# Merged mask matmuls and a later division in two attention blocks

## The chip, the cores and the metric

The kernel runs on one core of a Trainium2 chip. The metric is the device time of one launch in microseconds. The core has five engines with a queue each: TensorE (PE in the profile), VectorE (DVE), ScalarE (ACT), GpSimd (POOL) and SyncE (SP), which issues the transfers. Matmul results lie in PSUM, everything else on the chip in SBUF.

## The reference

Four blocks are applied in turn to `x` of 4 x 1024 x 128 (batches, tokens, channels). Each adds `s * silu(ffn(xn))` to `x`, where `xn` is the layer norm of `x` and `s` an attention or state-space result on `xn`:

```python
xn = _layernorm(x, axis=-1)
s = _L0_attn_ref(xn, ...)           # windowed causal attention, 16 heads of 8, window of 250 keys
g = _silu(_L0_ffn_ref(xn, ...))     # channel mix
x = x + s * g
xn = _layernorm(x, axis=-1)
s = _L1_attn_ref(xn, ...)           # causal attention, 16 heads of 8
g = _silu(_L1_ffn_ref(xn, ...))     # mixture of 8 experts
x = x + s * g
...                                 # block 2: full attention; block 3: state space and local attention
```

In blocks 0 and 1 a query at position t sees the keys up to t, in block 0 only the last 250 of them. Scores of other keys are masked before the softmax.

## The kernel before, in words

All of blocks 0 to 2 run through one function, `_attention`, with the mode `window`, `causal` or `full`. It works in units: a unit is one batch and four of the 16 heads (16 units per block). Tokens are cut into tiles of 128. A unit has two passes.

The first pass, `maxima`, finds the largest score of each query. For a query tile `qt` the queries lie on the 128 PSUM partitions and the keys along the row. PE multiplies `q9` with `k9` (bf16, results in `max_ps`), then adds the mask to the same PSUM words by a matmul of the identity `ident16` with a tile of 0 and -1e30 (`k.mask[mode]`). DVE reduces the row to a negative maximum, `neg` (L344). One `max_ps` tile is two PSUM banks, 1024 words a row, and there are two such buffers. It holds four heads where a head's keys fit into 256 words (query tiles 0 and 1, pitch 128 and 256), two heads at pitch 512 and one at pitch 1024. In window mode a head of query tile 2 or later has 384 keys. Both of its edges need masking: the first 134 keys and the last 128. Tile 0 has 128 keys, tile 1 has 256, of which the first 6 and the last 128 are masked. In causal mode only the last 128 keys are masked. POOL splits `neg` into three bf16 parts (`negp`), PE transposes them (`neg_ps`), DVE copies them out (`negr`), and three transfers on SP put them as rows into `q9`.

The second pass, `attend`, takes blocks of 128 keys against up to 512 queries (half `hf` 0 or 1 of the tokens). For each block and pair of heads PE computes scores (`sc`, one bank each), ACT takes the exponential into `pt` (L417), and POOL zeroes what lies beyond the edges (`keep`, L387). Two blocks later (`lag` is 2 in blocks 0 and 1, 1 in block 2) `values` multiplies by the values and accumulates in `o_ps`, of which there is a single buffer. After a half's last block, DVE copies `o_ps` to `os` (L448). Then `normalize` transposes `os` on PE to `ot`, and DVE takes the reciprocal of the sums (`rec`, L460) and multiplies (`at`, L461). `ot`, `sc`, `neg_ps` and several others share three PSUM slots of one bank each.

Units overlap. While unit n attends, the maxima of units n+1 and n+2 are computed. `_interleave` merges the lists of steps in a fixed ratio, together with the projections of the next batch and the layer norms and routing for the next block (`plan`). The end of a unit (its last values, the second half's division, and after a batch's last unit the four `finish` steps: transposition and output projection) is inserted into the next unit's list at fixed places. PE keeps this order exactly. The program's scheduler arranges DVE's and POOL's instructions among themselves.

```python
            def second(hn=hn, i=i):
                if i >= lag:
                    values(*blks[i - lag])
                pair.pop(hn)(1)
                if i > lag and blks[i - lag - 1][0] < blks[i - lag][0]:
                    normalize(0)
```

Here the first half is divided one block after its last values. The second half's division is inserted at place 5 of the next unit's list, its values at places 1 and 3.

The masks are built once at the start by POOL: a memset and one or two selects each (L1897, L1900), ahead of other memsets and of the first layer norm's `ln_rs`.

## Time and profile before

| | us |
|---|---|
| median of three runs | 3613.82 (3608.35 to 3614.92) |
| the profiled execution: its time | 3610.66 |
| its span in the profile | 3608.9 |
| PE busy with matmuls | 3138.7 (87%), 24592 of them |
| DVE busy | 2445.6 (68%) |
| ACT busy | 1988.7 (55%) |
| POOL busy | 1417.2 (39%) |
| mask matmuls of block 0 (`max_ps<-mask_window`) | 960, first at 67.2, last at 525.0 |
| mask matmuls of block 1 (`max_ps<-mask_causal`) | 512, first at 615.3, last at 1327.4 |

In the lines of the timeline the first number is the start in the span, the second the time from the first start to the last end of the merged instructions. A matmul's duration includes its drain, so several may be busy at once; the distance between starts tells how fast they stream. Square brackets tell how long the engine had been idle and what ended that. In the table by stretches the columns are busy us and instructions of each engine, then the granted TensorE clock (1 is full speed), the share of transfer time and GB/s. `PEld` is the weight load, which overlaps with matmuls.

### The profile page before, as it was taken

How to read it: one execution, taken by the hardware profiler on the slowest of the kernel's cores; microseconds unless marked ns; L12 is line 12 of the kernel's file. 1: busy time of each engine (PE TensorE's matmuls, PEld its weight loads, DVE VectorE, ACT ScalarE, POOL GpSimd, SP SyncE). 2: the span in 40 equal slices, each digit the busy share in tenths (PEclk: the TensorE clock that was granted, in tenths of full speed). 3: DMA queues.
4: the chain of work that ended last, by engine and by line, in shares of the span. 5: the costliest groups of instructions: out<-in, count | busy, mean ns of one | idle time of the engine just before them, and what ended most of it. 6: DMA issues, size and time to landing. Idle time of an engine off the chain costs nothing. (4 is left out here: it accounts for less than half of the span.)

```text
span 3608.9 us, 64740 instructions
## 1 busy us (share of the span) xinstructions
PE 3138.7 (87%) x24592; PEld 1704.4 (47%) x24729; DVE 2445.6 (68%) x4927; ACT 1988.7 (55%) x4191; POOL 1417.2 (39%) x1962
## 2 busy tenths in 40 slices
PE   4889889999898986899999989677499999989897
PEld 3545446654343433433323333223366666666665
DVE  7667664457777752788786766652587888778785
ACT  2444453346555552366665665554366666666674
POOL 5555552012323223030321300211576667656663
PEclk8999999999999997999999999888699999999999
DMA  3322312112222102011111221100210111010110
GB/s 99 71 60 55 70 42 83 46 33 51 57 42 57 34 22 69 21 44 28 41 34 33 55 53 31 33 19 9 78 22 18 21 25 24 18 25 22 29 26 21
DMA packets 133083, 146.09 MB, mean 40 GB/s; under 512 B 80403, under 2 KB 107931, under 8 KB 125467
## 3 DMA queue, kind: packets, MB, share of 16 engines
q1 hardware_dynamic: 130724, 137.75, 16.0%
q0 software_dynamic: 2048, 4.20, 0.4%
q8 instruction: 196, 3.21, 0.4%
q14 instruction: 115, 0.93, 0.1%
HBM read 93.83 MB, written 30.11 MB: 34 GB/s over the span
## 5 line engine op out<-in xcount | busy, mean ns | idle before, releaser
L417 ACT ACTIVATE pt<-sc 128x512 f32<-128x512 f32 (+3 forms) x2432 | 1077.0, 511 | 786.1 <-PE sc L78 737.7
L344 DVE TENSOR_REDUCE neg<-max_ps 128x1 f32<-128x1024 f32 (+6 forms) x1088 | 1177.9, 1102 | 477.2 <-PE max_ps L78 424.1
L78 PE MATMUL sc<-q,k 128*128 128x512 bf16 (+3 forms) x2403 | 651.8, 342 | 126.2 <-ACT pt L417 70.0
L78 PE MATMUL max_ps<-k,q 128*128 128x512 bf16 (+3 forms) x2198 | 625.0, 350 | 86.2 <-DVE neg L344 39.5
L78 PE MATMUL o_ps<-pt,va 128*32 128x512 f32 (+3 forms) x4864 | 560.6, 527 | 19.9 <-POOL pt L387 10.2
L387 POOL TENSOR_SCALAR_AFFINE_SELECT pt<-pt 128x256 f32<-128x256 f32 (+2 forms) x768 | 292.3, 399 | 568.2 <-ACT pt L417 566.3
L78 PEld LDWEIGHTS <-k 128*128 128x128 bf16 x2432 | 183.0, 98 | 544.2 <-issue 418.1
L78 PEld LDWEIGHTS <-q 128*128 128x128 bf16 x2304 | 222.7, 99 | 359.6 <-issue 241.2
L168 POOL CAST negp<-neg 128x32 bf16<-128x32 f32 x48 | 10.2, 212 | 719.3 <-DVE neg L344 719.2
L1603 ACT ACTIVATE pr<-lsc,nb,r 128x128 f32<-128x128 f32 x512 | 202.7, 476 | 61.2 <-DVE nb L1595 57.6
L1524 POOL TENSOR_TENSOR qn<-qn,rot 128x512 f32<-128x512 f32 x128 | 164.9, 1294 | 139.8 <-DVE rot L1516 125.9
L1533 POOL TENSOR_TENSOR rn<-ss,neghalf 128x16 f32<-128x16 f32 x64 | 188.9, 2951 | 68.8 <-DVE ss L1531 59.3
L78 PEld LDWEIGHTS o_ps<-pt,va 128*32 128x32 f32 x4864 | 99.7, 109 | 213.8 <-issue 160.3
L691 ACT ACTIVATE h<-hp,eb 128x512 f32<-128x512 f32 x128 | 80.9, 684 | 197.8 <-PE hp L78 190.2
L78 PEld LDWEIGHTS <-ident 128*128 128x128 bf16 x1472 | 146.2, 100 | 87.5 <-issue 22.7
L1441 PE MATMUL qk_ps<-wqkv,hT 128*128 128x512 f32 x256 | 137.9, 623 | 24.9 <-DVE hT L1487 10.3
L78 PE MATMUL hp<-xT,ew 128*128 128x512 f32 x256 | 130.3, 634 | 19.7 <-ACT rope_t L234 9.3
L701 DVE SCALAR_TENSOR_TENSOR xn<-op,gates,xn 128x128 f32<-128x128 f32 x256 | 72.1, 344 | 100.4 <-PE op L78 100.4
L78 PEld LDWEIGHTS op<-ew,h 128*128 128x128 f32 x1024 | 123.6, 192 | 20.1 <-issue 17.0
L78 PE MATMUL max_ps<-mask_window,ident 128*128 128x134 bf16 (+2 forms) x960 | 132.0, 221 | 0.0
L78 PE MATMUL op<-ew,h 128*128 128x128 f32 x1024 | 125.3, 276 | 0.0
L65 POOL TENSOR_TENSOR ln_rs<-ln_ve,neghalf 128x4 f32<-128x4 f32 x72 | 73.7, 1025 | 113.1 <-DVE ln_ve L63 109.7
(347 smaller groups left out, 5452.9 us busy)
## 6 DMA issues: line engine op xcount, KB each, us to landing
q<-qx SPq DMA_DIRECT2D x144, 192.0 KB
k<-kx SPq DMA_DIRECT2D x432, 64.0 KB
va<-vb SPq DMA_DIRECT2D x120, 128.0 KB
x<-x SPq DMA_DIRECT2D x20, 512.0 KB
qx<-qp SPq DMA_DIRECT2D x12, 768.0 KB
kx<-kp SPq DMA_DIRECT2D x12, 768.0 KB
ew<-in_e1w_dram SPq DMA_DIRECT2D x64, 128.0 KB
x<-in_x_dram SPq DMA_DIRECT2D x8, 512.0 KB
```

What stands on the lines that cost most here:

```text
L65: nc.gpsimd.tensor_tensor(rs, ve, k.neghalf[:, :n], ALU.pow)
L78: k.tc.keep_in_program_order(k.nc.tensor.matmul(*args, **kw))
L168: eng.tensor_copy(dst[:, 0], src)
L344: nc.vector.tensor_reduce(neg[:, j0 : j0 + m, qt0], of, AX.X, ALU.max, negate=True)
L387: nc.gpsimd.affine_select(out=pt, in_=pt, pattern=[[0, 2], [step, pt.shape[2]]], compare_op=ALU.is_ge, fill=0.0, base=base, channel_multip ...
L417: nc.scalar.activation(pt[:, j % 2, :width], sc[:, :width], AF.Exp, scale=scale)
L691: nc.scalar.activation(h[:, hh, :], hp[:, hh, :], AF.Gelu, bias=eb1[:, e, hh : hh + 1])
L701: nc.vector.scalar_tensor_tensor(to, op[:, c, :], gates[:, 4 * n + c, e : e + 1], to, ALU.mult, ALU.add)
L1441: pin(nc.tensor.matmul(*args, **kw))
L1524: nc.gpsimd.tensor_tensor(qn[:, i], qn[:, i], rot, ALU.add)
L1533: nc.gpsimd.tensor_tensor(rn, ss.rearrange("p w h -> p (w h)"), k.neghalf[:, : 2 * NH], ALU.pow)
L1603: nc.scalar.activation(t.pr[:, h, :], t.sc[r][:, c, :], AF.Exp, bias=t.nb[r][:, c : c + 1], scale=t.r8[:, h : h + 1])
```

## The change

The masks of a unit are added by fewer matmuls. For query tile 0, where four heads share a bank, one matmul adds the mask to all four (the mask is read four times by a step of zero). For tile 1, two heads share a bank and one matmul serves both; in window mode it covers all 256 keys of each. For window tiles from 2 on, one matmul per head writes the two edges as two runs of 134 words, 250 words apart. Both mask tiles are now allocated 512 columns wide in the pool `upto3`, and the causal mask is filled over 384 columns.

The division of a half moves one block of keys later in blocks 0 and 1 (`late` is 1 there, 0 in block 2): the first half's to the block after, the second half's from place 5 to place 7 of the next unit's list. The `finish` steps move by two places too.

```diff
+                pitch = parts[1][2] if len(parts) > 1 else 1024
...
-                        if masked:
-                            mw = min(c1 - c0, k.mask[mode].shape[1])
-                            W = k.mask[mode].shape[1]
-                            spans = [(W - P, W)]
-                            if W - mw < W - CONTEXT:
-                                spans.insert(0, (W - mw, W - CONTEXT))
-                            for m0, m1 in spans:
-                                matmul(
-                                    flat[:, at + c1 - c0 - W + m0 : at + c1 - c0 - W + m1],
-                                    lhsT=k.ident16,
-                                    rhs=k.mask[mode][:, m0:m1],
...
+                        if mode == "full" or c1 < hi or pitch < 512 and (place + pitch) % 512:
+                            continue
+                        mask = k.mask[mode]
+                        if mode == "window" and width == 3 * P:
+                            two = lambda a: a.rearrange("p (g c) -> p g c", c=CONTEXT)[:, :, 0 : 3 * P - CONTEXT]
+                            to, rhs = two(flat[:, at : at + 2 * CONTEXT]), two(mask[:, 0 : 2 * CONTEXT])
+                        else:
+                            heads = 512 // pitch if pitch < 512 else 1
+                            mw = width if mode == "window" else P
+                            b0 = at - at % 512 if pitch < 512 else at
+                            end = (c1 - c0) if pitch >= 512 else width
+                            to = flat[:, b0 : b0 + heads * end].rearrange("p (h c) -> p h c", h=heads)[:, :, end - mw : end]
+                            rhs = mask[:, 3 * P - mw : 3 * P].unsqueeze(1).to_broadcast([P, heads, mw])
+                        matmul(to, lhsT=k.ident16, rhs=rhs, start=False, stop=True, skip_group_check=True)
...
+    late = 0 if mode == "full" else 1
...
-                if i > lag and blks[i - lag - 1][0] < blks[i - lag][0]:
+                if i > lag + late and blks[i - lag - late - 1][0] < blks[i - lag - late][0]:
                     normalize(0)
...
-                for i in range(lag + 1):
-                    weights.insert(1 + 2 * i, late[i])
-                for i, step in enumerate(late[lag + 1 :]):
-                    weights.insert(min(len(weights), 2 * lag + 4 + 3 * i), step)
+                for i in range(lag):
+                    weights.insert(1 + 2 * i, left[i])
+                weights.insert(2 * lag + 1 + 2 * late, left[lag])
+                for i, step in enumerate(left[lag + 1 :]):
+                    weights.insert(min(len(weights), 2 * lag + 4 + 2 * late + 3 * i), step)
...
-    for name, width, reach in (("causal", P, None), ("window", 3 * P, CONTEXT)):
-        m = k.mask[name] = const.tile([P, width], BF16, name=f"mask_{name}")
+    for name, width, reach in (("causal", 3 * P, None), ("window", 3 * P, CONTEXT)):
+        k.mask[name] = upto3.tile([P, 4 * P], BF16, name=f"mask_{name}")
+        m = k.mask[name][:, 0:width]
```

More of the change, by code (lines that the diff above doesn't have):

```diff
@@ L315, in step @@
                         at = place + c0 - lo
-                        masked = mode != "full" and c1 == hi
                         matmul(
@@ L321, in step @@
                             start=True,
-                            stop=not masked,
+                            stop=mode == "full" or c1 < hi,
                             skip_group_check=True,
                         )
-                        if masked:
-                            mw = min(c1 - c0, k.mask[mode].shape[1])
-                            W = k.mask[mode].shape[1]
-                            spans = [(W - P, W)]
-                            if W - mw < W - CONTEXT:
-                                spans.insert(0, (W - mw, W - CONTEXT))
-                            for m0, m1 in spans:
-                                matmul(
-                                    flat[:, at + c1 - c0 - W + m0 : at + c1 - c0 - W + m1],
-                                    lhsT=k.ident16,
-                                    rhs=k.mask[mode][:, m0:m1],
-                                    start=False,
-                                    stop=m1 == W,
-                                    skip_group_check=True,
-                                )
+                        if mode == "full" or c1 < hi or pitch < 512 and (place + pitch) % 512:
[12 more added lines that the diff above has]
+                        matmul(to, lhsT=k.ident16, rhs=rhs, start=False, stop=True, skip_group_check=True)
                 j0, m = parts[0][0], len(parts)
@@ L526, in rest @@
         nonlocal steps, ending
-        late = []
+        left = []
         for n, (b, g) in enumerate(order):
@@ L545, in rest @@
                 streams.append((coming[:3], coming[3:7], coming[7:])[g])
-            if late:
-                for i in range(lag + 1):
-                    weights.insert(1 + 2 * i, late[i])
-                for i, step in enumerate(late[lag + 1 :]):
-                    weights.insert(min(len(weights), 2 * lag + 4 + 3 * i), step)
+            if left:
+                for i in range(lag):
[3 more added lines that the diff above has]
+                    weights.insert(min(len(weights), 2 * lag + 4 + 2 * late + 3 * i), step)
             _interleave(*streams, *plan.get(n, []))
-            late = closing + (finish(b) if g == 3 else [])
-        _run(late)
+            left = closing + (finish(b) if g == 3 else [])
+        _run(left)
     return begin, rest
```

## The prediction

> **What bounds the kernel now.** I read the table by stretches first, then the waits of TensorE (PE) in the two stages that the edit touches, then short timelines. Blocks 0 and 1 hold windowed attention (about 115 to 556 us) and causal attention (about 800 to 1364 us). The static order of the changed program differs from the old one in these two stages alone: from block 2 on every engine has the same order, and ACT's and SP's never change.

> ```profile
> core 0: us, PE busy (x) PEld busy (x) DVE busy (x) ACT busy (x) POOL busy (x), PEclk, DMA share, GB/s
> 180.00:270.00 90.00, 79.93 (x737) 43.66 (x736) 56.00 (x81) 41.70 (x125) 53.53 (x124) 0.98 0.27 60
> 810.00:900.00 90.00, 85.62 (x639) 37.24 (x648) 67.98 (x88) 54.09 (x132) 26.98 (x59) 1.00 0.24 51
> 2610.00:2700.00 90.00, 89.42 (x1094) 65.91 (x1086) 72.86 (x210) 55.53 (x133) 67.31 (x65) 0.96 0.11 24
> ```

> PE is the busiest engine of both stages (80 and 86 of 90 us), DVE comes next in the second. But PE's busy time includes the drain of its matmuls. Walking the trace from start to start, and counting each bf16 matmul at its column time (the timelines below), the streams fill 299 of the 415 us between 115 and 530, and 410 of the 550 between 780 and 1330. The rest is PE standing at the head of its queue. The profile names part of that, the window stage first, the causal stage second:

> ```profile
> PE sc L78 <- ACT pt L417: 14.6, 46, 0.6
> PE o_ps L78 <- POOL pt L387: 8.1, 5, 2.2
> PE ot L82 <- DVE os L448: 4.6, 4, 2.3
> ...
> PE sc L78 <- ACT pt L417: 15.6, 37, 3.0
> PE sc L78 <- DVE at L461: 13.7, 3, 4.6
> PE ot L82 <- DVE os L448: 3.6, 10, 0.6
> ```

> The columns are total us, times, longest. The change can reach the `ot` rows and the `at` row, not the `pt` rows, which are the larger.

> **Part 1, the masks.** Per unit (four heads; 16 units in each block) the windowed masks fall from 60 matmuls to 27, the causal ones from 32 to 27; with as many weight loads that is 608 matmuls and 608 loads fewer. What counts is columns:

> ```profile
> 123.55 0.27 PE L78 MATMUL max_ps<-k,q 128*128 128x256 bf16 x1
> 123.66 0.24 PE L78 MATMUL max_ps<-mask_window,ident 128*128 128x6 bf16 x2
> 123.74 0.27 PE L78 MATMUL max_ps<-k,q 128*128 128x256 bf16 x1
> ...
> 301.47 0.33 PE L78 MATMUL max_ps<-k,q 128*128 128x384 bf16 x1
> 301.63 0.28 PE L78 MATMUL max_ps<-mask_window,ident 128*128 128x134 bf16 x2
> 301.75 0.33 PE L78 MATMUL max_ps<-k,q 128*128 128x384 bf16 x1
> ```

> From one head's score to the next is 0.28 us: 0.16 for 384 columns and 0.12 for masks of 134 and 128. So a mask streams at 0.42 ns per column plus about 2.5 ns, and its weight load is hidden.
> - Query tiles 2 to 7 (24 heads per unit): 262 columns in two matmuls, 114 ns, become 268 in one, also 114 ns. Nothing.
> - Tile 0: four masks of 128 become one of 512. Nothing (-6 ns).
> - Tile 1: from head to head is 0.19 us, 0.76 for four. After, four scores of 0.109 and two masks of 512 columns, 0.216 each: 0.87. So +0.11 us per unit, +1.7 us over 16: the merged mask also streams the zeros.
> - Causal: the same columns everywhere, five matmuls fewer per unit, -0.2 us in all.

> The masks are also built at the start: the causal one grows from 128 to 384 columns, so its memset from 0.20 to 0.41 us and its select from 0.29 to 0.50 (the rows of the window mask). POOL runs without a gap from there to the first `ln_rs` at 16.72, for which DVE waits: +0.4 us on the path. Sum of part 1: +1.9 us.

> [...] No row here writes two runs. The nearest reads them: the `shift_ps` matmuls fetch 4 runs of 64 fp32 and take 379 ns for 256 columns, as do those of `o_ps` whose 256 are contiguous (379). [...] I take the row: 0 ns. [...]

> [...]

> **Part 2, the division.** `os` is copied by DVE out of `o_ps`, then PE transposes it (`ot`), then DVE divides (`rec`, `at`) and only then is the PSUM slot of `ot`, one of three that scores use, free. The second half's division is issued in the next unit right after its last value block, so PE meets a copy that is not done:

> ```profile
> 509.99 0.49 PE L78 MATMUL sc<-q,k 128*128 128x384 bf16 x2
> 512.76 0.63 PE L82 MATMUL ot<-ident,os 128*128 128x128 f32 x4 [2.27 <-DVE os L448]
> ```

> Before this `ot` PE stood still for 2.4 us. Taking the 62 divisions of the two blocks that have a unit's matmuls behind them from start to start, waits on the copy are 5.8 us in block 0 (2.4, twice 1.1, 0.6, the rest under 0.15) and 6.8 us in block 1 (0.3 in ten units, 0.6 to 0.8 in five). A block of keys later, at two to three reductions' distance (0.95 us each), the copy (0.68 us) is done: all 12.6 us go from this place. What is late next is DVE itself: behind the lost wait the next `max_ps` (two buffers) needs a reduction, and around 820 to 826 us DVE has no idle time at all. So I count half: -6.3 us. The range of this term is 0 to -12.6; beyond it little, as the copy itself is not moved.

> The first half's division waits elsewhere. Three times in block 1 the layer norm for the next block fills DVE ahead of `rec`, and scores wait for the slot:

> ```profile
> 979.74 1.07 PE L78 MATMUL o_ps<-pt,va 128*32 128x512 f32 x8
> 985.37 1.03 PE L78 MATMUL sc<-q,k 128*128 128x512 bf16 x2 [4.56 <-DVE at L461]
> ```

> After, `ot` stands behind this pair of scores, so the pair runs in the gap. The next thing is a `max_ps`, both buffers of which wait for the same DVE: its first reduction ends at 984.81 (start 984.13, 0.68), and PE goes on there. Gained: 0.56 us, and the pair's 0.45 us: 1.0 us, three times, -3 us. Not -14.

> DVE's `rec` and `at` (0.55 us) now come behind `negr` in most windowed units, not ahead of it. The three SP transfers that `negr` feeds start that much earlier; scores wait for them 1.6 us in block 0 and 3.5 us in block 1. I take -1 us. POOL swaps a `keep` of 0.42 us with `negp` in some units; `negp` is ready 1.6 to 17 us ahead of its transpose in all units but the first two of block 0 and the last of block 1, so nothing. The four `finish` steps of a batch (16 matmuls and four DVE instructions) move with the division; nothing in the next unit needs them, so 0.

> **Sum.** +1.9 - 6.3 - 3 - 1 = -8.4 us. The profiled execution took 3610.66 us (span 3608.9), so 3602.3 on its scale. It was 3.2 us below the median of the runs, 3613.82, so 3605.4 on that of the median.

> **The rivals.**
> - All of it comes back: PE alone sets the pace, 12.6 + 3 + 3, less 1.9: -17 us, 3597. For it: DVE is idle over 30% in the window stage. Against: the waits on `pt` follow PE directly and are untouched.
> - The waits only move: every `ot` wait reappears as `max_ps` on `neg` or `sc` on `pt`, and the masks cost their 1.9 us: -1 to +2, about 3614. For it: DVE's unbroken run at 820 to 826 us.
> [...]
> - The scheduler gives DVE's instructions a new place after the edit (order of `rec`, `neg`, `at`): in three windowed units `rec` falls behind a 1.22 us addition, holding a slot that much longer: +1 to +3 us inside the range of the first case.

> **How the numbers follow.** A measurement of this kernel can tell about 0.2%, 7.2 us, from no change. Half of the waits returned, 3605 (3600 to 3610): 47%, of which somewhat over half beyond 0.2%. All returned, 3597: 15%. Waits moved, 3614: 18%. Slow masks, 3620 to 3648: 20%. Faster 0.26 + 0.15 + 0.01 = 0.42; same 0.20 + 0.16 = 0.36; slower 0.20 + 0.02 = 0.22. The range 3593 to 3625 leaves out the upper part of the slow masks and little below.

> **What would show it.** Right: the 2x134 mask at about 277 ns, the next score 0.114 us after its start; no `ot` row on `os` in either stage; `sc` on `at` gone, with a `max_ps` on `neg` of some 3.5 us three times instead; both stages 3 to 5 us shorter, the rest equal. Wrong: a next score over 0.13 us after a 2x134 mask; an `ot` that still waits; a change outside the two stages.

## The result and the profile after

The changed kernel takes 3587.74 us (median of 4 runs, 3583.56 to 3588.59) against 3612.71 for the kernel before beside it: ratio 0.993, 95% interval 0.9917 to 0.9943. That is 25 us less; the forecast was 8 less. Its profiled execution has a span of 3581.8 us.

The two attention stages that the edit touches, and the next one, from the first score to the last transpose of a division. First the table by stretches of the kernel before, then that of the changed one (columns as in the prediction; the first number pair is the stretch, then its length):

```profile
core 0: us, PE busy (x) PEld busy (x) DVE busy (x) ACT busy (x) POOL busy (x), PEclk, DMA share, GB/s
107.70:556.40 448.70, 397.63 (x3642) 219.46 (x3640) 287.40 (x510) 221.50 (x656) 250.45 (x605) 0.96 0.27 58
777.90:1364.10 586.20, 530.56 (x3812) 230.29 (x3847) 405.64 (x639) 341.20 (x790) 173.45 (x355) 0.98 0.18 42
1514.30:2494.20 979.90, 863.35 (x4664) 305.54 (x4749) 663.06 (x853) 610.15 (x1135) 197.13 (x204) 0.97 0.14 34
```

```profile
core 0: us, PE busy (x) PEld busy (x) DVE busy (x) ACT busy (x) POOL busy (x), PEclk, DMA share, GB/s
109.00:545.90 436.90, 389.17 (x3163) 199.62 (x3161) 285.83 (x510) 222.38 (x656) 249.33 (x605) 0.99 0.26 59
771.70:1343.00 571.30, 521.96 (x3778) 226.85 (x3777) 404.49 (x639) 340.09 (x790) 172.89 (x355) 0.98 0.19 44
1489.30:2459.90 970.60, 865.98 (x4750) 302.26 (x4749) 662.04 (x853) 610.01 (x1135) 196.79 (x204) 0.98 0.14 34
```

Block 0 is 11.8 us shorter, block 1 14.9, and block 2, in which nothing was edited and every engine's order is the same, 9.3. (Elsewhere the two profiles differ the other way: the stretch between blocks 0 and 1 is 4 us longer, all behind block 2 is 7 us longer. So the stages of one pair of profiles do not simply add up to the gain.) Look at the clock column too: 0.96 became 0.99 in block 0. The waits of TensorE in the changed kernel, block 0, then block 1 (us in total, times, longest):

```profile
PE sc L78 <- ACT pt L418: 18.7, 57, 0.5
PE max_ps L78 <- DVE neg L344: 5.5, 4, 2.0
PE o_ps L78 <- POOL pt L388: 5.4, 6, 1.1
PE o_ps L78 <- DVE os L449: 3.7, 2, 1.8
...
PE sc L78 <- ACT pt L418: 21.3, 55, 3.0
PE max_ps L78 <- DVE neg L344: 18.2, 18, 3.6
PE o_ps L78 <- DVE os L449: 2.4, 3, 0.8
...
PE ot L82 <- DVE os L449: 0.8, 1, 0.8
```

The `ot` row on `os` has all but gone (0.8 us, once in each block), the `sc` row on `at` (13.7 us, three times) is not there any more, and `max_ps` on `neg` has come up. In the kernel before that row read, in block 0 and in block 1:

```profile
PE max_ps L78 <- DVE neg L344: 4.2, 3, 2.0
...
PE max_ps L78 <- DVE neg L344: 0.7, 2, 0.4
```

Three of the 18 waits that block 1 now has there are the layer norm's (below); the other 15 will matter. The new mask matmul in its two runs (timeline):

```profile
296.00 0.32 PE L78 MATMUL max_ps<-k,q 128*128 128x384 bf16 x1
296.17 0.28 PE L78 MATMUL max_ps<-mask_window,ident 128*128 128x268 bf16 x1
296.28 0.33 PE L78 MATMUL max_ps<-k,q 128*128 128x384 bf16 x1
```

It takes 0.28 us and the next score starts 0.11 us after it, which is what the prediction's rate gives for 268 columns in one run (0.114 us). One of the three places in block 1 where the layer norm fills VectorE:

```profile
971.09 0.60 PE L78 MATMUL sc<-q,k 128*128 128x512 bf16 x2
971.53 0.60 PE L82 MATMUL ot<-ident,os 128*128 128x128 f32 x4
975.71 0.48 PE L78 MATMUL max_ps<-k,q 128*128 128x384 bf16 x1 [3.58 <-DVE neg L344]
...
976.09 0.53 PE L78 MATMUL max_ps<-k,q 128*128 128x384 bf16 x1
```

The scores now run ahead of the stop, and the stop is 3.58 us where it was 4.56. What the prediction had not looked at stands in the last line: the same 384-column matmul that takes 0.33 us above takes 0.53 here. After the stop TensorE runs at half its clock: from 975.7 to 979.1 the granted clock is 0.50. The stop of the kernel before, by stretches of about 3.4 us:

```profile
978.00:981.40 3.40, 2.66 (x21) 0.98 (x19) 2.23 (x11) 1.78 (x4) 1.78 (x2) 1.00 0.24 88
981.40:984.90 3.50, 0.00 (x0) 0.00 (x0) 3.46 (x22) 0.00 (x0) 1.47 (x2) 1.00 0.43 150
984.90:988.30 3.40, 2.93 (x10) 1.33 (x11) 2.46 (x4) 1.67 (x4) 0.52 (x1) 0.53 0.00 0
988.30:991.70 3.40, 3.35 (x27) 1.33 (x27) 1.75 (x2) 2.05 (x6) 0.81 (x2) 0.97 0.00 0
```

Here a stretch without matmuls is followed by one at clock 0.53 (the stretches do not lie exactly on the clock's records in the trace, of which the one at 0.50 goes from 985.1 to 988.5). So by an estimate from these rows this stop cost its idle time and then up to 1.7 us (half) of the next 3.4.

### The profile page after: what moved, and what is told of

The parts are those of the page before. It is cut to its first block, busy times and chain, and to the rows that moved or that the text cites. A ratio compares the mean times of both kernels' runs of the same rounds, so it can differ in the third digit from the quotient of the medians.

```text
span 3581.8 us, 63638 instructions
## 1 busy us (share of the span) xinstructions
PE 3132.4 (87%) x24121; PEld 1680.5 (47%) x24121; DVE 2443.2 (68%) x4927; ACT 1988.3 (56%) x4191; POOL 1415.4 (40%) x1962
## 5 line engine op out<-in xcount | busy, mean ns | idle before, releaser
L78 PE MATMUL sc<-q,k 128*128 128x512 bf16 (+3 forms) x2432 | 650.4, 340 | 105.2 <-ACT pt L418 75.1
L78 PE MATMUL max_ps<-k,q 128*128 128x512 bf16 (+3 forms) x2304 | 634.5, 349 | 104.7 <-DVE neg L344 58.6
L78 PE MATMUL o_ps<-pt,va 128*32 128x512 f32 (+3 forms) x4864 | 556.7, 523 | 14.4 <-POOL pt L388 7.3
L78 PEld LDWEIGHTS <-k 128*128 128x128 bf16 x2432 | 185.8, 98 | 542.7 <-issue 409.7
L78 PEld LDWEIGHTS <-q 128*128 128x128 bf16 x2304 | 217.2, 99 | 379.6 <-issue 245.1
L78 PEld LDWEIGHTS o_ps<-pt,va 128*32 128x32 f32 x4864 | 99.4, 108 | 225.1 <-issue 166.7
L78 PE MATMUL hp<-xT,ew 128*128 128x512 f32 x256 | 129.8, 632 | 19.3 <-ACT rope_t L234 8.9
L78 PEld LDWEIGHTS op<-ew,h 128*128 128x128 f32 x1024 | 123.0, 192 | 19.7 <-issue 16.5
L78 PE MATMUL max_ps<-mask_window,ident 128*128 128x268 bf16 (+1 forms) x432 | 126.5, 293 | 0.0
L78 PE MATMUL op<-ew,h 128*128 128x128 f32 x1024 | 124.9, 275 | 0.0
L78 PEld LDWEIGHTS <-ident 128*128 128x128 bf16 x864 | 85.4, 99 | 72.3 <-issue 31.6
```

The lines of the kernel that those rows point to most:

```text
L78: k.tc.keep_in_program_order(k.nc.tensor.matmul(*args, **kw))
```

## The experiments

Where nothing else is said, each kernel is compared with the kernel before, run beside it on the same chip (medians of 3612 to 3614 us).

**The two parts alone.** In `masks_only` the changed kernel has its division in the old place; `division_only` is the kernel before with the later division and the old masks.

```diff
-    late = 0 if mode == "full" else 1
+    late = 0
```

> The changed kernel with the division at its old place (late = 0 everywhere): the merged masks alone. Theory A (the waits at the division bring the gain, columns are what a mask costs): +2 us against before, 3612 to 3617. Theory B (fewer matmuls and loads count for themselves): most of the 25 us, under 3600. Theory C (the gain is time at half the TensorE clock, and any shift of the program changes it): anything between, with the half-clock time of stages that are not edited changed by 10 us or more.

> The kernel before with only the division moved a block of keys later in blocks 0 and 1; masks as before. Theory A: 3588 to 3594, nearly all of the gain. Theory B: 3605 to 3610. Theory C: under 3600, with less half-clock time in block 0 than the 34 us of before.

Measured: the masks alone 3612.49 us, ratio 1.0001 (0.9993 to 1.0009); the division alone 3588.57, ratio 0.9936 (0.9921 to 0.995). All of the gain is the division's, and 608 matmuls fewer are worth nothing that these runs could tell (3 us).

**A later start.** The kernel before with one or two more memsets on POOL at the start, each 1.2 us, to see whether any shift in time moves the rest by several us:

```diff
+            nc.gpsimd.memset(k.va[1], 1.0)
```

> The kernel before with one more POOL memset of 1.2 us ahead of the first layer norm, so that all of PE's work starts 1.2 us later and nothing else is changed. Theories A and B: +1.2 us, 3614. Theory C: the windows in which the clock is granted fall elsewhere, so the time moves by something else, 5 us or more either way, and the half-clock time of unedited stages changes.

> The same with two more memsets, 2.4 us later. Theories A and B: +2.4 us, 3615. Theory C: another value again, not on a line with the run before.

Measured: 3614.73 and 3615.42, both 1.0007 (0.9998 to 1.0015). A shift as such gives no gain. Their profiles, though, show that single executions differ: the stage between blocks 0 and 1 takes 220 to 222 or 226 us, and all behind block 2 takes 1115 to 1122, whatever the kernel.

**One half, one block.** `first_half_later` leaves the second half's division in its old place, `second_half_later` the first half's; `window_block_only` and `causal_block_only` set

```diff
+    late = 1 if mode == "window" else 0
```

and the same with "causal". All have the old masks.

> The kernel before with its old mask matmuls; only the division of the first half of each unit in blocks 0 and 1 comes a block of keys later, that of the second half stays where it was. Waits theory (the gain is the time for which TensorE stood at a division's transposes and behind them): the two halves' parts add up to the 24 us that both gave, so this run and its partner lie at 3588 to 3612 and their gains sum to 24, plus or minus 4; the first half's division stands in the middle of a unit with few columns to stream beside it, so about half, 3600. Clock theory (a stop at a division only counts when it takes a window of 3.4 us under the share at which the clock is halved, and one stop removed lifts such a window as well as two): each half alone gives most of the gain, 3590 to 3596, and the two gains sum to well over 24.

> The kernel before with its old mask matmuls; only the division of the second half of each unit in blocks 0 and 1 (the one that runs inside the next unit, and the finishing steps of a batch after it) comes later. Waits theory: the rest of the 24 us, 3600, and the three long waits on `at` in block 1 (13.7 us) go here, so if the halves differ this one gives more, down to 3595. Clock theory: 3590 to 3596, as for the first half alone.

> The kernel before with its old mask matmuls; both divisions come later in block 0 (the window mode) alone. Waits theory: block 0 shorter by 12 us, nothing else, 3600.5. If block 2's 7 us follow from what runs ahead of it by its phase against the clock's windows, block 2 can be anywhere between 971 and 979 here though its code is untouched, and the time is 3593 to 3601. If block 2's gain needs the later division in block 1, block 2 stays at 979.

> The kernel before with its old mask matmuls; both divisions come later in block 1 (the causal mode) alone. Waits theory: block 1 shorter by 14 us, nothing else, 3598.5. If block 2's 7 us are handed on from block 1, they appear here and not in the run with block 0 alone: 3591. If they are a matter of phase, either run can have them or not.

Measured: first half 3604.64, ratio 0.9976 (0.9966 to 0.9985); second half 3601.07, 0.9972 (0.9962 to 0.9983); block 0 alone 3608.56, 0.998 (0.9971 to 0.9988); block 1 alone 3599.62, 0.9956 (0.9943 to 0.997). The halves sum to 0.52%, 19 us, the blocks to 0.64%, 23 us: about additive, and no half gives most of it. That is what the waits theory said; the clock theory's 3590 to 3596 for each half is out. Which waits gave the gain is not told by that yet. Two details came out otherwise than expected: block 0 alone gave 7 us, not 12, and the three long waits on `at` went with the first half's division (they are gone in its trace and unchanged in that of `second_half_later`). Block 2 took 977 to 980 us in all four profiles.

**Block 2.** Is its gain handed on, or an accident? Just ahead of its first scores TensorE waits for maxima, and in the kernel before block 2 starts at the half clock. `block_2_stream_filled` (kernel before) fills that wait with needless transposes; `block_2_stop_longer` (division later, old masks) makes it 1.2 us longer:

```diff
-    begin += steps[:lead]
...
+        x, y = steps[lead - 2 : lead]
+        begin += steps[: lead - 2] + [lambda: (fill(12), x()), lambda: (fill(4), y())]
```

```diff
-                nc.vector.tensor_reduce(neg[:, j0 : j0 + m, qt0], of, AX.X, ALU.max, negate=True)
+                again = 2 if mode == "full" and n == 1 and qt0 == 2 and j0 == 1 else 1
+                for _ in range(again):
+                    nc.vector.tensor_reduce(neg[:, j0 : j0 + m, qt0], of, AX.X, ALU.max, negate=True)
```

> The kernel before, with 16 needless transposes (the identity into a spare bank) put where TensorE stands 2.0 us just ahead of block 2's first scores, waiting for VectorE's maxima; all else stands in the same order, and nothing waits for the spare bank. Clock theory: the 3.4 us window there is no longer under the share, the half clock at block 2's start goes (3.4 us of it in each of the eight profiles of kernels in which block 2 took 977 to 980 us), block 2 then runs 970 to 973 as in the two profiles without it, and the time falls by up to 7 us: 3605 to 3610. Waits theory: no wait was taken away, so nothing changes, 3612 to 3614, or plus 1 to 2 us for the extra work.

> The kernel with the later division and the old masks (3588), with one maximum just ahead of block 2's first scores reduced twice: one more 1.2 us instruction on VectorE, once in the whole run, for which TensorE stands 1.2 us longer. Clock theory: the window there falls under the share, block 2 starts at the half clock and comes back to 977 to 980 us: plus 6 to 9 us, 3594 to 3597. Waits theory: plus 0 to 1.2 us, 3588 to 3590.

By stretches, the start of block 2 (1514.3) in the kernel before:

```profile
1510.20:1513.60 3.40, 1.58 (x8) 0.55 (x6) 3.40 (x7) 1.06 (x1) 0.00 (x0) 1.00 0.00 0
1513.60:1517.00 3.40, 3.06 (x6) 1.35 (x7) 2.42 (x3) 1.96 (x3) 0.00 (x0) 0.58 0.00 0
```

The same filled, then with the longer stop (it begins at 1518.3 and at 1495.0):

```profile
1514.20:1517.60 3.40, 3.22 (x24) 2.45 (x24) 3.40 (x7) 1.06 (x1) 0.00 (x0) 1.00 0.00 0
1517.60:1521.00 3.40, 2.97 (x9) 1.16 (x9) 2.53 (x3) 2.18 (x3) 0.00 (x0) 1.00 0.02 5
```

```profile
1490.20:1493.60 3.40, 0.78 (x4) 0.19 (x2) 3.40 (x6) 1.06 (x1) 0.00 (x0) 1.00 0.00 0
1493.60:1497.00 3.40, 2.64 (x6) 1.37 (x6) 2.88 (x3) 1.28 (x1) 0.00 (x0) 0.50 0.00 0
```

The clock did what was expected both times: 1.00 where the stream was filled, 0.50 behind the longer stop. In the profiles block 2 went from 979.9 to 973.6 us, and from 972.1 to 974.9. But the whole time did not follow: 3612.49, ratio 0.9994 (0.9987 to 1.0001), and 3587.77, 0.9935 (0.9919 to 0.995), the ratio of `division_only`. I had expected up to 7 us less and 6 to 9 more; that step was wrong. Block 2 varies between 970 and 980 us, and the clock is what varies: in the ten profiles whose trace has all matmul records TensorE stands still for 201 to 204 us of it each time, while the half clock adds anything from 6 to 17. A change at its start does not fix the rest.

**Twice the copy.** If the wait for `os` is the matter, a longer copy must cost more in the old place. Kernel before, and division later:

```diff
+                if mode != "full":
+                    nc.vector.tensor_copy(os, o)
                 nc.vector.tensor_copy(os, held.pop(("o", hf)))
```

> The kernel before, with the copy of the value sums into `os` (0.68 us) made twice in blocks 0 and 1, 64 times in all. Where TensorE stands at a division's transposes it stands 0.68 us longer, and where it nearly stood it begins to. Waits theory: about 25 to 45 of the 64 divisions now show the wait, plus 17 to 31 us: 3629 to 3643. Clock theory: the longer stops put more windows under the share at which the clock is halved, so the loss is larger than the added waits, with more time at the half clock in blocks 0 and 1 than the 34 and 27 us of before.

> The same doubled copy in the kernel with the division a block later (old masks; 3588 without the second copy). Waits theory: a division now has a whole block of keys between its copy and its transposes, so the second copy is hidden there, and what it costs is VectorE's 44 us of extra work where `max_ps` waits for `neg`: plus 3 to 12 us, 3591 to 3600, well under half of what it costs in the old place. If the later division only shifted which stop shows, it costs as much as in the old place, 17 to 31 us.

Measured: 3661.3, ratio 1.013 (1.011 to 1.015), and 3623.87, 1.0031 (1.0022 to 1.004): plus 48 us in the old place, plus 35 with the later division. Both are over what either theory gave. TensorE's waits for the copy in blocks 0 and 1, first the old place, then the later division:

```profile
PE ot L82 <- DVE os L450: 22.6, 16, 3.5
...
PE o_ps L78 <- DVE os L450: 10.6, 11, 2.6
...
PE ot L82 <- DVE os L450: 27.1, 16, 2.1
...
PE o_ps L78 <- DVE os L450: 11.2, 12, 1.7
```

```profile
PE o_ps L78 <- DVE os L451: 10.6, 11, 2.6
...
PE ot L82 <- DVE os L451: 5.2, 4, 1.5
...
PE o_ps L78 <- DVE os L451: 11.6, 12, 1.7
...
PE ot L82 <- DVE os L451: 2.5, 2, 1.5
```

At the transposes the second copy adds 40 us in the old place (from 5.4 and 4.4) and about 6 with the later division (from 0.8 and 0.8): there the distance hides it, as expected. What I had left out is the bank `o_ps`. It has one buffer, so the next half's first values wait for the copy wherever the division is: plus 7.5 to 9 us in each block, in both kernels. The clock theory had one thing right: in the old place TensorE was at the half clock for 42 and 31 us of the two blocks, against 34 and 27, which is some 6 of the 48 us. Still open after that: does the copy's place in the chain matter, or VectorE's load?

**The copy on ScalarE, shared, and the division later still.** The old place (`copy_on_scalar_old_place`) and the later one (`copy_on_scalar_later`) with

```diff
-                nc.vector.tensor_copy(os, held.pop(("o", hf)))
+                copy = nc.vector.tensor_copy if mode == "full" else nc.scalar.copy
+                copy(os, held.pop(("o", hf)))
```

`copy_shared_later` gives 256 columns to each engine, and `two_blocks_later` sets `late = 2` in blocks 0 and 1.

> The kernel before, with the 64 copies into `os` of blocks 0 and 1 made by ScalarE (0.6 us each by its 128x512 rows) in place of VectorE. Load theory (VectorE's queue is nearly the bound there): VectorE loses 43.6 us of work, of which about 0.75 was on the path by the doubled copy, and ScalarE is busy for only 50 to 59% of these stages: minus 15 to 33 us, 3580 to 3598. Chain theory (the transposes wait for the copy whoever makes it): the copy now stands behind the exponentials in ScalarE's queue, 0.5 to 0.6 us each, so it is no earlier: 3605 to 3630.

> The same with the division a block later (3588 with VectorE's copy). Load theory: another 10 to 30 us less, 3558 to 3578. Chain theory: at the transposes almost nothing is waited for any more (1 to 2 us), what is left is the bank `o_ps` (5.5 us) and now ScalarE's exponentials come 0.6 us later at each half: 3585 to 3600.

> The later division, and each copy of blocks 0 and 1 shared: 256 columns by VectorE, 256 by ScalarE, at the same time. Load theory: half of what the whole move gives, 3573 to 3583. Chain theory: only the 5.5 us at the bank `o_ps` get shorter, by half: 3584 to 3588.

> The later division of blocks 0 and 1 put two blocks of keys after the old place in place of one, VectorE's copy as it was (3588 for one block). At the transposes 1.6 us are still waited for, the rest of the waits for the copy is at the bank `o_ps` and does not depend on the division's place. Chain theory: minus 0 to 2 us, 3586 to 3589. Load theory: no load is changed, the same. If the gain came from the distance as such, in proportion, another 10 to 24 us less.

Measured:

| | us | ratio | block 0 | block 1 | block 2 |
|---|---|---|---|---|---|
| ScalarE, old place | 3602.46 | 0.9969 (0.996 to 0.9978) | 447.2 | 576.1 | 979.8 |
| ScalarE, later | 3592.02 | 0.994 (0.9919 to 0.9961) | 438.3 | 568.4 | 980.3 |
| shared, later | 3598.75 | 0.9965 (0.9951 to 0.9979) | 441.7 | 575.3 | 979.6 |
| two blocks later | 3589.3 | 0.9941 (0.992 to 0.9963) | 435.0 | 581.3 | 980.3 |

With the later division VectorE loses 36 us of busy time in the two stages (690 to 654) and the time is the same as `division_only`: a lighter VectorE alone does not shorten the whole, and the load theory is out. In block 1 the waits of `max_ps` on `neg` did fall, from 18.2 us (18 times) to 11.8 (5 times), so the short ones among them go back to the copy in VectorE's queue. But the waits of scores on `pt` rose from 21.6 to 25.3 us, and the stage became only 4 us shorter. In the old place ScalarE's copy gives 10 us, nearly all in block 1, where its waits now read

```profile
PE sc L78 <- ACT pt L417: 19.0, 42, 3.0
PE sc L78 <- DVE at L462: 14.1, 3, 4.7
...
PE ot L82 <- ACT os L449: 1.4, 2, 0.7
```

The wait for the copy is down from 4.4 us to 1.4, but the three waits on `at` stay; those only the later division removes. (I had expected ScalarE's copy to come no earlier than VectorE's. It does.) The shared copy missed both ranges, 10 us above the later division: `o_ps` is freed only when both engines have read it, and it now waits on ScalarE for 4.1 and 8.4 us. Two blocks gave no more than one in the whole; by stages block 0 gained 3 us and block 1 lost 10, in a profiled execution that was itself 10 us above the median of its runs.

**The better of each stage.** The changed kernel with `late` 2 in block 0 and 1 in block 1, and block 1's copies by ScalarE:

```diff
-    late = 0 if mode == "full" else 1
+    late = {"window": 2, "causal": 1, "full": 0}[mode]
-                nc.vector.tensor_copy(os, held.pop(("o", hf)))
+                copy = nc.scalar.copy if mode == "causal" else nc.vector.tensor_copy
+                copy(os, held.pop(("o", hf)))
```

> The changed kernel with the division two blocks later in block 0 (one in block 1) and block 1's copies into `os` made by ScalarE. If the stages add up: block 0 435 and block 1 568, together 7 us less than the mean of the three profiles at 3588 (438 and 572), so 3581 plus or minus 5, of which block 2 at 980 in place of 971 to 975 would take 5 to 9 back: 3586. If the two stages' times were accidents of phase: 3585 to 3593.

Measured: 3581.65 us, ratio 0.9917 (0.9903 to 0.9931), with block 0 at 435.5, block 1 at 568.6 and block 2 at 976.1. The stages add up. It is the fastest kernel of the study; its interval overlaps that of the changed kernel (0.9917 to 0.9943), against which it was not run side by side.

## Why the prediction was wrong, and where it was right

To compare stages I split each one's length in the trace into three: the matmuls' column time at full clock (from start to start, fp32 counted double: in the two profiles 512 columns take 0.43 us in fp32 and 0.216 in bf16), what the half clock adds to it, and the rest, TensorE standing. The standing is put down to whatever released the matmul that ended it. This also counts the short pauses that the profile's wait rows leave out because the drain of the matmul before covers them. Means, in us, over the profiles with the division in the old place (five for block 0; three for block 1, those whose trace has all matmul records) and in the new place one block later (three; two):

| | block 0, old | block 0, new | block 1, old | block 1, new |
|---|---|---|---|---|
| half clock adds | 14.1 | 6.0 | 11.3 | 9.8 |
| standing | 116.9 | 112.4 | 134.1 | 122.0 |
| of it, transposes on the copy `os` | 6.2 | 1.0 | 7.3 | 1.0 |
| scores on `at` | 0 | 0 | 14.2 | 0 |
| on VectorE's maxima `neg` | 5.1 | 7.5 | 8.1 | 25.9 |
| on ScalarE's `pt` | 37.7 | 41.0 | 50.6 | 42.0 |
| on POOL's `pt` | 10.4 | 8.6 | 2.8 | 3.2 |
| all else | 57.5 | 54.3 | 51.1 | 49.9 |

Standing fell by 4.5 + 12.1 = 16.6 us, the half clock's share by 8.1 + 1.5 = 9.6. The two stages together became 25 us shorter, as much as the medians (column time rose by 1). Half of what fell under "all else" is waits for transfers in block 0, which vary from run to run. Against the prediction's sum:

| us | forecast | measured |
|---|---|---|
| masks | +1.9 | 0, within 3 |
| waits on the copy | -12.6 | -11.5 |
| of these, again at VectorE's maxima | +6.3 | +9.0 |
| three layer-norm stops | -3 | -3.0 |
| waits on `pt`, ScalarE's and POOL's | 0 | -6.7 |
| all other waits (`negr` among them) | -1 | -4.4 |
| half clock | 0 | -9.6 |

- **The step that failed: "The change can reach the `ot` rows and the `at` row, not the `pt` rows, which are the larger."** It put the waits on `pt` at nothing ("untouched"). They fell by 6.7 us. In block 1 those on ScalarE fell by 8.6, half of it at scores and half at other tiles (`tr_ps`, `at_ps`, `wo_ps`, `rt_ps`) that wait for one of the PSUM slots that scores use too. In block 0 those on ScalarE rose by 3.3, and those on POOL fell by 1.8. What happened on POOL can be seen. Twice in block 0 it multiplies `xn` for 2.35 us, and the values wait for a `keep` behind that. First the kernel before, then the changed one:

```profile
260.77 0.42 POOL L387 TENSOR_SCALAR_AFFINE_SELECT pt<-pt 128x268 f32<-128x268 f32 x1
261.15 2.35 POOL L87 TENSOR_TENSOR xn<-s,xn 128x1024 f32<-128x1024 f32 x1
...
264.28 0.96 PE L78 MATMUL o_ps<-pt,va 128*32 128x384 f32 x4 [2.20 <-POOL pt L387]
...
264.90:268.30 3.40, 3.40 (x23) 1.64 (x22) 0.96 (x1) 0.99 (x5) 1.71 (x6) 0.50 0.02 5
```

```profile
259.62 1.14 POOL L388 TENSOR_SCALAR_AFFINE_SELECT pt<-pt 128x268 f32<-128x268 f32 x3
260.73 2.35 POOL L87 TENSOR_TENSOR xn<-s,xn 128x1024 f32<-128x1024 f32 x1
...
263.64 1.14 PE L78 MATMUL o_ps<-pt,va 128*32 128x256 f32 x8 [1.11 <-POOL pt L388]
...
263.60:267.00 3.40, 2.94 (x28) 1.26 (x29) 0.50 (x1) 1.02 (x4) 2.98 (x11) 1.00 0.00 0
```

  Three `keep` instructions now stand ahead of the multiplication, not one; the stop is half as long, and the clock behind it is 1.00 in place of 0.50. The order on POOL is the new one in `second_half_later` and the old one in `first_half_later`, so it comes with the second half's division. Why the shared slots come free sooner in block 1 is not shown.
- **A term that was put at nothing without a reason: the half clock, 9.6 us.** The prediction showed the clock column and read nothing from it. In the kernel before the clock was halved for 34 us of block 0 and 27 of block 1. In all nine kernels whose second half is divided in the old place in block 0, two to four windows of 3.4 us at the half clock come behind these stops on POOL; of the ten with the later place, nine have none and one has one. Of the six windows that block 0 lost on average, three are these. The others come and go with where a stop falls on the clock's grid (counted in the last section). No run changed the clock alone in block 0, so the size of this term is read from the split.
- **"So I count half: -6.3 us" was right in kind and still too hopeful.** The copy's waits were measured rightly, and VectorE was next, as the prediction said: four fifths of these waits appeared again at its maxima. In ten units of block 1 the pause before one `max_ps`, counted from start to start, grew from 0.31 to 0.76 us (the row below shows 0.59, without the drain):

```profile
815.25 0.68 DVE L449 COPY os<-o_ps 128x512 f32<-128x512 f32 x1
815.85 2.81 DVE L344 TENSOR_REDUCE neg<-max_ps 128x1 f32<-128x768 f32 x3
...
816.85 0.54 PE L78 MATMUL max_ps<-k,q 128*128 128x512 bf16 x2 [0.59 <-DVE neg L344]
```

  TensorE no longer stands at the transposes for this copy; it stands at the reduction behind it. In `second_half_later` the exchange in block 1 is complete: 6.3 us less on the copy, 6.9 more on the maxima. The rival in which all 12.6 us are gained (3597) came nearest to the measured time by luck: most of these waits appeared again, and others that it did not name fell.
- **The three layer-norm stops:** right in kind and size. Three waits of 4.56 us on `at` became three of up to 3.6 on `neg`, 1 us less each, as forecast.
- **The masks:** +1.9 us forecast, 0 measured (within 3 us). Column time in block 0 did grow, by 2.9 us (with the later division, from 319.0 with the old masks to 321.9), but the whole time did not. The two runs of 134 cost nothing: at full clock 115 ns pass in the changed kernel from such a mask to the next matmul (median of 375), and in the kernel before it was 58 for the mask of 134 columns and 56 for that of 128. No run shows the cost of writing two runs on which the 20% for slow masks, 3620 to 3648, stood. And 608 matmuls fewer gave 0 (within 3 us).
- **"A change outside the two stages" was to show the prediction wrong.** Block 2 changed by 9.3 us in the profile, but not by the edit: with the division later it took 970.6, 972.1 and 974.9 in three kernels, and 980 in `copy_on_scalar_later`, `copy_shared_later` and `two_blocks_later`; with the division in the old place it took 973.6 once its start was filled. A profile is one execution, and here a stage without an edit moved by nearly as much as an edited one.
- **`negr` earlier, -1 us:** in the profiles scores wait for it in block 1 1.7 us in place of 3.5; in block 0 it was 1.6 before and 4.5 after. Nothing can be made of that.
- **What stays open:** what shortens the waits for the shared slots in block 1, what places block 2's stops against the clock's windows from run to run, and so how much of the 25 us in a single run is block 2's.

## What to carry to other kernels

When a wait is taken off the engine that sets the pace, look for it at the next thing that this engine needs: here four fifths of it appeared again there. Do not leave the larger rows out of the sum because the edit does not name them: ask which slots and which queues the moved instructions share with them. Add to each stop what it does to TensorE's clock just behind it: here the half clock's share was 9.6 of the 25 us. And before reading a gain off a single profile, look how far stages without an edit moved.

## What the runs showed of the hardware

Stops of 2 us were enough in some places: in the kernel before, the 2.20 us up to 264.28 shown above lie ahead of a window at 0.50 from 264.9. So were runs of 16 matmuls of 8 columns (`rt_ps`, 0.11 us from start to start): in the kernel before they start at 317.7, in a window filled to 0.26, and the next one, from 319.5, is at 0.50. In the changed kernel the same 16 start at 312.9, in a window filled to 0.42, and the clock stays at 1.00.
